# A graph layer on one core: the node layer's own-row product is made early, and two node batches are in flight at the end

## The chip, the cores and the metric

The kernel runs on one core of a Trainium2 chip. A core has a matrix engine (PE, with PEld as the name for its weight loads), a vector engine (DVE), a scalar engine (ACT), a general engine (POOL) and an engine that only issues transfers and waits (SP). Each runs its own instructions strictly in order, and they meet through semaphores. The metric is device time in microseconds, the median of several runs; lower is better.

## The reference

12500 nodes with 64 features, 212500 edges sorted by destination, and one message-passing layer before a residual. The edges are grouped by `row` (the reference's `src` argument) for the sum.

```
h = relu(layernorm(x))                                  # 12500 x 64
edge_in = concat([h[src], h[dst], dist])                # 212500 x 129
e   = silu(edge_in @ eW1 + eb1)                         # 212500 x 128
e   = silu(e @ eW2 + eb2)                               # 212500 x 128
agg = segment_sum(e, src, 12500)                        # 12500 x 128
out = silu(concat([h, agg]) @ nW1 + nb1) @ nW2 + nb2    # 12500 x 64
return x + out
```

The last line but one is the node layer. Its first product has two parts: `h @ nW1[:64]`, which needs only a node's own row, and `agg @ nW1[64:]`, which needs the finished sum.

## The kernel before, in words

All arithmetic on PE is in f32, apart from small helper products. Nodes are laid out as 125 per "bucket" (`L`), 100 buckets (`NB`), and four buckets (`G`) make a batch, so there are 25 batches of 500 nodes. Work runs in these stages:

- **Tables.** `normed`, `turned` and `products` make the normalised rows `h`, transpose them (`hr`), write them to DRAM as `hd` (L678), and write `h @ eW1`'s two halves as tables `ta` and `tb`. These steps are generators; a chain of them called `feed` is advanced a little at a time between other work.
- **Edges, in 208 blocks of 1024.** For each block, `count` finds on DVE and PE the place of every edge, and `send` builds its rows on PE (`qp`, L429), copies them on ACT (`qs`, L439) and scatters them by eight indirect DMAs that POOL issues (L452, 1661 in all) into a DRAM array `q`, sorted by batch and rank.
- **Sweeps.** Once a "level" of ranks is complete in `q`, its 25 batches are swept, one to two steps each, 450 steps in twelve levels. The last four levels have one step a batch. A step loads `qt` (edge rows, L503) and `a` (own rows, L512) through SP, and does on PE: `lr` (L528), `pt` (L542 and L548), `p` (the second layer, L580) and `seg` (the sum over edges, L594). DVE makes one-hot matrices `oneT` (L533) and `one` (L561) and adds `seg` into `aggT` (L605). ACT does the two SiLUs and a bias copy.
- **Tail.** In the last level, `s_add` appends to a list `tails` a generator `nodes(B, ...)` for each finished batch. It does the node layer: `z` on PE from `aggT` (L246) and from the own rows `hrn`, loaded from `hd` (L249), SiLU into `zs` on ACT (L251), `o` on PE (L255), `os` = `o` plus the residual `xr` on DVE (L258), and the store (`rows16`, L120).

PE, DVE, ACT and SP run the order in which the code writes their instructions (`manual_schedule`); POOL's is the planner's. The order of a step is written out in a list, and each `None` in it is a "hook", at which pieces of sending, up to two turns of `feed`, and one turn of the first tail are put in:

```python
turn = [
    (s_pt, 1), (s_add, -2), (s_one_t, 2), None, (s_bias, 1), (s_p2, 0), (s_one, 0), None, (s_seg, -1), None, (s_lr, 3), None,
]
```

The number beside a function says how many steps ahead of the current one, k, it works. So in one step of the last level `z`, `o`, `os` and the store of the batch two back stand at the four hooks.

Loads for batch k+4 are put on SP by `fetch`, called at the end of `s_one(k)`. In the last level `fetch` also calls `nodes_in`, which loads the residual rows `xr` and the own rows `hrn`. `xr` and `hrn` have six buffers each (`nd_in`, `NQ + 2`). A load into a buffer waits on SP until the last reader of its old contents is done, and whatever SP has to issue after it waits too. The PSUM pool `mm` has four buffers, used in turn by `qp`, `lr`, `pt`, `z` and `o`.

Of the kernel before, what the change touches and what calls it, by code (L numbers as in the profile page):

```python
# [28 lines left out]
F32 = mybir.dt.float32  # L29
# [3 lines left out]
AF = mybir.ActivationFunctionType  # L33
OP = mybir.AluOpType
# [4 lines left out]
P = 128  # L39
L = 125  # L40
# [11 lines left out]
G = 4  # L52
# [9 lines left out]
FIRST = 4  # L62
# [11 lines left out]
def tile_gnn(ctx: ExitStack, tc: tile.TileContext, x, src, dst, ew, eW1, eb1, eW2, eb2, nW1, nb1, nW2, nb2, out):  # L74
    nc = tc.nc
# [41 lines left out]
    def rows16(dma, to, of):  # L117

        for part in (slice(0, 112), slice(112, L)):
            dma(to[part], of[part])  # L120
# [86 lines left out]
            nc.scalar.copy(to.rearrange("l (i a) h -> l a i h", a=2)[:, a], abs_[a])  # L207

    hd = dram.tile([P, NB // 2, P], F32, name="hd")
    bkE = const.tile([P, 2 * TB, NP], F32, name="bkE")  # L210
    locE = const.tile([P, 2 * TB, NP], F32, name="locE")
    offE = const.tile([P, 2 * TB, NP], F32, name="offE")
# [17 lines left out]
    def nodes_in(B, sb):  # L230
        b = B * G
        xr = sb.tile([L, G, D], F32, name="xr")
        rows16(nc.sync.dma_start, xr, x_rows[:, b : b + G, :])
        nc.gpsimd.tensor_tensor(xr, xr, nb2b[:L, None, :].to_broadcast([L, G, D]), op=OP.add)
        hr = sb.tile([P, G // 2, P], F32, name="hrn")
        nc.sync.dma_start(hr, hd[:, b // 2 : b // 2 + G // 2, :])
        return xr, hr

    def nodes(B, xr, hr, ps, sb, tag):

        b = B * G

        zs = sb.tile([P, 2, G // 2, L], F32, name="zs")
        z = [ps.tile([P, G // 2, L], F32, name="z", tag=tag) for _ in range(2)]
        for a in range(2):
            nc.tensor.matmul(z[a], w1g, aggT[:, b + a : b + G : 2, :], start=True, stop=False)  # L246
        for a in range(2):
            half = slice(a * D, (a + 1) * D)
            nc.tensor.matmul(z[a], w1n[half, :], hr[half, :, :L], start=False, stop=True)  # L249
        for a in range(2):  # L250
            nc.scalar.activation(zs[:, a], z[a], AF.Silu, bias=nb1c)  # L251
        yield
        o = ps.tile([L, G, D], F32, name="o", tag=tag)
        for t in range(G):
            nc.tensor.matmul(o[:, t, :], zs[:, t % 2, t // 2, :], w2n, start=True, stop=True)  # L255
        yield
        os_ = sb.tile([L, G, D], F32, name="os")
        nc.vector.tensor_tensor(os_, o, xr, op=OP.add)  # L258
        yield
        rows16(nc.sync.dma_start, out_rows[:, b : b + G, :], os_)  # L260


    NQ = 4
# [5 lines left out]
    with ExitStack() as work:  # L269
# [496 lines left out]
        def scale(p0, p1):  # L766

            v = bkE[:, :, p0:p1]

            q4 = lp.tile([P, 2 * TB, p1 - p0], F32, name="q4", tag=f"q4{p0}")  # L770
            nc.vector.tensor_scalar(q4, v, 0.5 - G / 2 - 1.0, 1.0 / G, op0=OP.add, op1=OP.mult)
            nc.vector.tensor_scalar(q4, q4, float(3 * 2**22), None, op0=OP.add)
            yield
            nc.vector.tensor_scalar(q4, q4, -float(3 * 2**22), None, op0=OP.add)
            nc.vector.scalar_tensor_tensor(offE[:, :, p0:p1], q4, float(ROWS * G - G), v, op0=OP.mult, op1=OP.add)
            scaled.update(range(p0, p1))
# [36 lines left out]
        with tc.tile_pool(name="lists", bufs=1, side="right") as lp:  # L813
            x0 = lp.tile([P, NE, D], F32, name="x0")
            x0_rows = x[: NE * P, :].rearrange("(j p) d -> p j d", p=P)
            nc.sync.dma_start(x0[:, :G, :], x0_rows[:, :G, :])
            srcR = lp.tile([NP, PAIR], I32, name="srcR")
            dstR = lp.tile([NP, PAIR], I32, name="dstR")
            f, sf = (lp.tile([NP, PAIR], F32, name=n) for n in ("f", "sf"))
            srcE = lp.tile([P, 2 * TB, NP], F32, name="srcE")  # L820
            fv = f.rearrange("p (g e) -> p g e", e=QR)
            lo = lp.tile([NP, 2 * NQR], F32, name="lo")
            steps15 = lp.tile([P, 2 * NQR], F32, name="steps15")
            nc.vector.tensor_scalar(steps15, nodes1[:, : 2 * NQR], 1.0, float(STEP), op0=OP.subtract, op1=OP.mult)
            rowsD = lp.tile([NP, NQR, 2, QR], BF16, name="rowsD")
            nc.vector.memset(srcR[96:NP, LAST:], N)
            vec = lambda v, lo_, n, m: bass.AP(tensor=v.tensor, offset=v.offset + lo_, ap=[[m, n], [1, m]])
            for to, v, queue in ((dstR, dst, nc.scalar), (srcR, src, nc.sync)):
                for p0, p1 in ((0, 96), (96, NP - 1)):
                    queue.dma_start(to[p0:p1, :], vec(v, p0 * PAIR, p1 - p0, PAIR))  # L830
                queue.dma_start(to[NP - 1 : NP, :LAST], vec(v, (NP - 1) * PAIR, 1, LAST))
            last = bass.AP(tensor=dst.tensor, offset=dst.offset + E - FEW, ap=[[PAD, 1], [0, PAD // FEW], [1, FEW]])
            nc.scalar.dma_start(dstR[NP - 1 : NP, LAST:].rearrange("p (r e) -> p r e", e=FEW), last)
            root = lp.tile([1, 1], F32, name="root")
            nc.scalar.activation(root, ones[:, :1], AF.Sqrt)
            nc.sync.dma_start(x0[:, G:, :], x0_rows[:, G:, :])
            extra_rows(nc.sync.dma_start)
            near, far = norm(x0[:, :G, :], G, True), norm(x0[:, G:, :], NE - G)
            places, table = destinations(), first_rows(0)
            next(near)  # L840
            next(places)
            list(near)
            next(table)
            next(places)
            nc.scalar.copy(sf[:, :BLK], srcR[:, :BLK])
            list(table)
            nc.scalar.copy(sf[:, BLK:], srcR[:, BLK:])
            list(places)
            load_rows(0)
            load_rows(1)  # L850
            next(far)
            list(by_edges())
            list(sources(0, FIRST))
            list(scale(0, FIRST))
            load(0)
            counting = count(0)
            next(counting)
            todo = groups()
            list(counting)
            load(1)  # L860
            for _ in range(2):
                list(todo.pop(0))
            sending = send_all(0, 2 * FIRST)
            feed = itertools.chain(far, *(first_rows(g) for g in range(G, NE, G)))
            for _ in range(2 * PIECES):
                next(sending)
                for _ in range(2):
                    next(feed, None)
            list(feed)
            windows(1)  # L870
            feed = itertools.chain(sources(FIRST, NP), scale(FIRST, NP), checks(), turns(todo, 3))
            for _ in sending:
                for _ in range(4):
                    next(feed, None)
# [31 lines left out]
        for k in range(first, len(steps) + 2):  # L906
            for s in turn:
                if s is None:
                    while len(marks) > 1 and at >= marks[1][0]:
                        marks.pop(0)  # L910
                    if len(marks) > 1:
                        (t0, n0), (t1, n1) = marks[:2]
                        goal = n0 + (n1 - n0) * (at + 1 - t0) / (t1 - t0)
                        while done + 1 <= goal + 0.001:
                            next(pieces, None)
                            done += 1
                    at += 1
                    for _ in range(2):
                        if not ndp and next(feed, 0) == 0:
                            feeding.close()  # L920
                            for name, bufs in (("nd_in", NQ + 2), ("nd", 2)):
                                ndp.append(work.enter_context(tc.tile_pool(name=name, bufs=bufs, side="right")))
                    if tails and next(tails[0], 0) == 0:
                        tails.pop(0)
                else:
                    f, ahead = s
                    if 0 <= k + ahead < len(steps):
                        f(k + ahead)
        for t in tails:
            for _ in t:  # L930
                pass


    flag_i = const.tile([1, 1], I32, name="flag_i")
# [9 lines left out]
    with tc.If(flag > 0):  # L944
        general_sums(tc, N, E, NB, H, src, dst, ew, ta, tb, aggT, w1d, eb1b, w2, ident, ones, eb2r, part)
        with tc.tile_pool(name="fin", bufs=2) as fin, tc.tile_pool(name="fps", bufs=4, space=PSUM) as fps:
            for B in range(NB // G):
                for _ in nodes(B, *nodes_in(B, fin), fps, fin, "fps"):
                    pass


def general_sums(tc, N, E, NB, H, src, dst, ew, ta, tb, aggT, w1d, eb1b, w2, ident, ones, eb2r, part):
# [120 lines left out]
```

## Time and profile before

| what | us |
|---|---|
| median of three runs (lowest, highest) | 2463.26 (2462.79, 2467.51) |
| the profiled execution, its own time | 2461.7 |
| its span, first to last instruction | 2459.9 |
| PE busy in the span | 2045.2 (83%) |
| DVE busy | 1936.9 (79%) |
| POOL busy | 1705.5 (69%) |
| ACT busy | 1088.8 (44%) |

The profiled execution's time and its span differ by 1.8 us, and it is 1.6 us below the median of the runs. A share of busy time is a mean over stages that have different limits, so the stages have to be looked at one by one. PE's busy time includes matmuls that overlap in its pipeline. The mean granted PE clock was 0.92 over the span and 1.00 in the stretches after 1600 us.

### The profile page before, as it was taken

What the parts mean: (1) busy time and instruction counts of PE and PEld (TensorE: products, weight loads), DVE (VectorE), ACT (ScalarE), POOL (GpSimd) and SP (SyncE); (2) the same over time, 40 slices, a digit from 0 to 9 for tenths busy, and PEclk for the clock granted to TensorE, in tenths of its full rate; (3) what the DMA queues carried; (4) which work ended last, traced back from release to release, by engine and by line L of the source; (5) the groups of instructions that cost most, each with busy time, mean ns of one, the idle gap of its engine ahead of it and who ended that gap; (6) DMA issues with size and microseconds to landing.
All of it is one profiled execution on the core that took longest, in us unless ns stands there. A gap on an engine that the chain in (4) does not pass through costs nothing.

```text
span 2459.9 us, 46292 instructions
## 1 busy us (share of the span) xinstructions
PE 2045.2 (83%) x16191; PEld 1829.8 (74%) x16191; DVE 1936.9 (79%) x3006; ACT 1088.8 (44%) x2403; POOL 1705.5 (69%) x1712
## 2 busy tenths in 40 slices
PE   3673776665688898898998988899999999999997
PEld 2452665555587787787887877888888898999986
DVE  7895777676787898787888788898889899886432
ACT  2452333222344454454544444454555555554442
POOL 4777777777777777777777777777777777762110
PEclk9575898877899999999999998999999999999999
DMA  4563566555666765667654544455555556665652
GB/s 116 185 217 124 168 186 193 183 175 171 210 212 211 219 210 180 215 215 227 194 166 165 166 156 161 154 182 165 177 172 181 179 166 207 215 199 174 193 162 67
DMA packets 237006, 443.85 MB, mean 180 GB/s; under 512 B 49804, under 2 KB 108735, under 8 KB 236561
## 3 DMA queue, kind: packets, MB, share of 16 engines
q1 hardware_dynamic: 158629, 269.79, 35.9%
q0 software_dynamic: 53536, 123.03, 14.3%
q10 hardware_dynamic: 24602, 47.98, 6.7%
q8 instruction: 132, 2.16, 0.4%
q14 instruction: 107, 0.88, 0.1%
HBM read 251.07 MB, written 189.55 MB: 179 GB/s over the span
## 4 chain that ended last, share of the span: by engine, by line
PE 36%; DMA 17%; DVE 16%; POOL 13%; issue 8%; ACT 2%; DVEq 0%; POOLq 0%; ACTq 0%; SPq 0%
DMA q<-qs,to 16%; POOL q L452 13%; PE seg L594 8%; PE pt L548 8%; PE p L580 7%; PE pt L542 4%; PE qp L429 4%; DVE oh L354 2%; DVE each L362 2%; DVE oneT L533 2%; PE lr L528 2%; DVE aggT L605 2%; DVE one L561 2%; DVE mine L404 1%; DVE rank L406 1%
## 5 line engine op out<-in xcount | busy, mean ns | idle before, releaser
L452 POOL DMA_INDIRECT q<-qs,to x1661 | 1676.4, 1009 | 586.3 <-issue 396.9
L552 ACT ACTIVATE e<-pt 128x512 f32<-128x512 f32 x450 | 268.7, 597 | 849.8 <-PE pt L548 839.2
L594 PE MATMUL seg<-one,e 128*128 128x125 f32 x3600 | 504.0, 285 | 110.2 <-DVE aggT L605 77.7
L594 PEld LDWEIGHTS seg<-one,e 128*128 128x128 f32 x3600 | 456.0, 199 | 140.0 <-issue 84.7
L580 PEld LDWEIGHTS p<-w,e 128*128 128x128 f32 x3600 | 472.3, 197 | 37.4 <-issue 17.8
L548 PE MATMUL pt<-oneT,a 125*128 125x128 f32 (+1 forms) x2400 | 487.1, 338 | 15.3 <-DVE oneT L533 15.3
L580 PE MATMUL p<-w,e 128*128 128x128 f32 x3600 | 494.1, 281 | 0.0
L548 PEld LDWEIGHTS pt<-oneT,a 125*128 125x128 f32 x2400 | 366.9, 200 | 35.4 <-DVE oneT L533 18.2
L439 ACT COPY qs<-qp 128x512 f32<-128x512 f32 x416 | 224.9, 588 | 356.8 <-PE qp L429 310.1
L533 DVE TENSOR_SCALAR oneT<-lr,part 125x512 f32<-125x512 f32 x450 | 335.0, 745 | 43.4 <-PE lr L528 42.8
L362 DVE TENSOR_REDUCE each<-oh 128x100 bf16<-128x800 bf16 x208 | 315.9, 1519 | 7.2
L561 DVE TENSOR_TENSOR one<-nodes,qt 128x500 f32<-128x500 f32 x450 | 302.4, 672 | 0.2 <-issue 0.2
L542 PE MATMUL pt<-ident,qt 128*128 128x128 f32 x1800 | 287.6, 285 | 1.3 <-DVE oneT L533 1.3
L429 PE MATMUL qp<-win,pick 64*128 64x256 f32 x1662 | 266.3, 435 | 24.2 <-DMA pick<-in_edge_weight_dram 9.1
L584 ACT ACTIVATE e<-p 128x512 f32<-128x512 f32 x450 | 268.7, 597 | 28.7 <-PE p L580 28.7
L574 ACT COPY p<-b2f 128x512 f32<-128x512 f32 x450 | 267.2, 594 | 0.0
L605 DVE TENSOR_TENSOR aggT<-aggT,seg 128x500 f32<-128x500 f32 x275 | 184.0, 669 | 65.5 <-PE seg L594 62.7
L408 DVE SCALAR_TENSOR_TENSOR to<-rank,offE 128x8 int32<-128x8 f32 x208 | 36.2, 174 | 251.3 <-DMA q<-qs,to 246.5
L429 PEld LDWEIGHTS qp<-win,pick 64*128 64x128 f32 x1662 | 162.5, 203 | 81.1 <-issue 44.3
L542 PEld LDWEIGHTS pt<-ident,qt 128*128 128x128 f32 x1800 | 200.7, 148 | 21.3 <-issue 13.4
L406 DVE TENSOR_REDUCE rank<-mine 128x8 f32<-128x800 f32 x208 | 205.1, 986 | 7.2
L404 DVE TENSOR_TENSOR mine<-oh,counts 128x800 f32<-128x800 bf16 x208 | 203.9, 980 | 8.3 <-PE counts L389 8.0
(145 smaller groups left out, 1454.3 us busy)
## 6 DMA issues: line engine op xcount, KB each, us to landing
qt<-q SPq DMA_DIRECT2D x150, 576.0 KB
a<-ta SPq DMA_DIRECT2D x300, 256.0 KB
qt<-q SPq DMA_DIRECT2D x150, 288.0 KB
q<-zeros ACTq DMA_DIRECT2D x25, 1080.0 KB
q<-qs,to POOLq DMA_INDIRECT x1661
q<-zeros ACTq DMA_DIRECT2D x10, 1440.0 KB
bc<-dests SPq DMA_DIRECT2D x103, 128.0 KB
win<-tb SPq DMA_DIRECT2D x416, 30.0 KB
```

Of the source, the lines that this page charges most:

```text
L362: nc.vector.tensor_reduce(each, oh.rearrange("p t b -> p b t"), AX.X, OP.add)
L429: nc.tensor.matmul(qps[i][:, t, : n_of[t]], pick[at, t * P : (t + 1) * P], win[at, : n_of[t]], start=True, stop=True)
L452: ins = nc.gpsimd.indirect_dma_start(out=q[:], out_offset=bass.IndirectOffsetOnAxis(ap=to[:k, j : j + 1], axis=0), in_=qs[:k, t, a, :], in ...
L533: nc.vector.tensor_scalar(oneT, st[k].pop("lr")[:L], part1[:L, :], None, op0=OP.is_equal)
L542: nc.tensor.matmul(pt[:, t, :], qt[:, j, :H], ident, is_transpose=True, start=t == 0, stop=False, skip_group_check=True)
L548: nc.tensor.matmul(pt[:, cols, :], a[:L, b, :], oneT[:, cols, :], start=False, stop=True, skip_group_check=True)
L552: nc.scalar.activation(e1, pt, AF.Silu)
L561: nc.vector.tensor_tensor(one.rearrange("p (b j) l -> p b j l", j=n), nodes1[:, None, None, :].to_broadcast(wide), loc[:, tiles[0][1] : ti ...
L574: nc.scalar.copy(p2, b2f)
L580: nc.tensor.matmul(p2[:, t, :], e1[:, t, :], w2, start=False, stop=t == G - 1, skip_group_check=True)
L584: nc.scalar.activation(e2, p2, AF.Silu)
L594: nc.tensor.matmul(item[2][:, b, :], e2[:, t, :], one[:, t, :], start=j < G, stop=j >= G * (n - 1))
```

## The change: what it does

The own-row product leaves the tail. A new generator `node_part` does for each batch: load `hrn` from `hd`, let six turns go by, two matmuls with `w1n` into two PSUM tiles of pool `mm`, two ACT copies to SBUF, and a store to a new DRAM array `zd` a turn later. The 25 generators stand at the end of `feed`, three at a time. In the program's order the first five batches' products come before the first `lr` of the sweeps and the other twenty in the first eighteen steps of 450.

In the tail, `nodes_in` loads `zh` from `zd` (128 x 500 f32) in place of `hrn` (128 x 256 f32). `nodes` has `z` from `aggT` alone; at its next turn DVE adds `zh` to the two halves of `z`, and ACT makes one SiLU over both. The result store is put off: `os` goes on a list, and the list is sent after the next batch's `z` matmuls. At each hook only one of the two first tails is advanced, by the parity of the hook, so that a batch takes two steps and two are in flight: in one step the new batch has its `z` at the first hook and its additions and SiLU at the third, and the batch before it has its `o` at the second and its `os` at the fourth.

```diff
+    zd = dram.tile([P, NB // G, 2, G // 2, L], F32, name="zd")
...
-        hr = sb.tile([P, G // 2, P], F32, name="hrn")
-        nc.sync.dma_start(hr, hd[:, b // 2 : b // 2 + G // 2, :])
-        return xr, hr
+        zh = sb.tile([P, 2, G // 2, L], F32, name="zh")
+        nc.sync.dma_start(zh, zd[:, B])
+        return xr, zh
+
+    def node_part(B, ps, sb, tag):
+        b = B * G
+        hr = sb.tile([P, G // 2, P], F32, name="hrn")
+        nc.sync.dma_start(hr, hd[:, b // 2 : b // 2 + G // 2, :])
+        for _ in range(6):
+            yield
+        z = [ps.tile([P, G // 2, L], F32, name="zp", tag=tag) for _ in range(2)]
+        for a in range(2):
+            half = slice(a * D, (a + 1) * D)
+            nc.tensor.matmul(z[a], w1n[half, :], hr[half, :, :L], start=True, stop=True)
+        zh = sb.tile([P, 2, G // 2, L], F32, name="zn")
+        for a in range(2):
+            nc.scalar.copy(zh[:, a], z[a])
+        yield
+        nc.sync.dma_start(zd[:, B], zh)
+        yield
+
+    unsent = []
+
+    def send_out():
+        while unsent:
+            rows16(nc.sync.dma_start, *unsent.pop(0))
...
-        zs = sb.tile([P, 2, G // 2, L], F32, name="zs")
+        zs = sb.tile([P, 2, G // 2, L], F32, name="zs", bufs=3)
...
-            nc.tensor.matmul(z[a], w1g, aggT[:, b + a : b + G : 2, :], start=True, stop=False)
+            nc.tensor.matmul(z[a], w1g, aggT[:, b + a : b + G : 2, :], start=True, stop=True)
+        send_out()
+        yield
         for a in range(2):
-            half = slice(a * D, (a + 1) * D)
-            nc.tensor.matmul(z[a], w1n[half, :], hr[half, :, :L], start=False, stop=True)
-        for a in range(2):
-            nc.scalar.activation(zs[:, a], z[a], AF.Silu, bias=nb1c)
+            nc.vector.tensor_tensor(zs[:, a], z[a], zh[:, a], op=OP.add)
+        nc.scalar.activation(zs, zs, AF.Silu, bias=nb1c)
         yield
...
         nc.vector.tensor_tensor(os_, o, xr, op=OP.add)
-        yield
-        rows16(nc.sync.dma_start, out_rows[:, b : b + G, :], os_)
+        unsent.append((out_rows[:, b : b + G, :], os_))
...
-            feed = itertools.chain(sources(FIRST, NP), scale(FIRST, NP), checks(), turns(todo, 3))
+            later = turns([node_part(B, mm, fp, "mm") for B in range(NB // G)], 3)
+            feed = itertools.chain(sources(FIRST, NP), scale(FIRST, NP), checks(), turns(todo, 3), later)
...
-                    if tails and next(tails[0], 0) == 0:
-                        tails.pop(0)
+                    if tails:
+                        both = tails[at % 2 :: 2][:1] if len(tails) > 1 else tails[:1] * (at % 2)
+                        for t in both:
+                            if next(t, 0) == 0:
+                                tails.remove(t)
...
+        send_out()
```

More of the change, by code (lines that the diff above doesn't have):

```diff
@@ L234, in nodes_in, with nodes @@
         nc.gpsimd.tensor_tensor(xr, xr, nb2b[:L, None, :].to_broadcast([L, G, D]), op=OP.add)
+        zh = sb.tile([P, 2, G // 2, L], F32, name="zh")
[3 more added lines that the diff above has]
+        b = B * G
         hr = sb.tile([P, G // 2, P], F32, name="hrn")
         nc.sync.dma_start(hr, hd[:, b // 2 : b // 2 + G // 2, :])
-        return xr, hr
-    def nodes(B, xr, hr, ps, sb, tag):
+        for _ in range(6):
[14 more added lines that the diff above has]
+            rows16(nc.sync.dma_start, *unsent.pop(0))
+    def nodes(B, xr, zh, ps, sb, tag):
         b = B * G
-        zs = sb.tile([P, 2, G // 2, L], F32, name="zs")
+        zs = sb.tile([P, 2, G // 2, L], F32, name="zs", bufs=3)
         z = [ps.tile([P, G // 2, L], F32, name="z", tag=tag) for _ in range(2)]
         for a in range(2):
-            nc.tensor.matmul(z[a], w1g, aggT[:, b + a : b + G : 2, :], start=True, stop=False)
+            nc.tensor.matmul(z[a], w1g, aggT[:, b + a : b + G : 2, :], start=True, stop=True)
+        send_out()
+        yield
         for a in range(2):
-            half = slice(a * D, (a + 1) * D)
-            nc.tensor.matmul(z[a], w1n[half, :], hr[half, :, :L], start=False, stop=True)
-        for a in range(2):
-            nc.scalar.activation(zs[:, a], z[a], AF.Silu, bias=nb1c)
+            nc.vector.tensor_tensor(zs[:, a], z[a], zh[:, a], op=OP.add)
+        nc.scalar.activation(zs, zs, AF.Silu, bias=nb1c)
         yield
@@ L949, in tile_gnn @@
                     pass
+            send_out()
 def general_sums(tc, N, E, NB, H, src, dst, ew, ta, tb, aggT, w1d, eb1b, w2, ident, ones, eb2r, part):
```

## The prediction

> **What bounds the kernel now.** I read the page's head, then busy time by stretch, then what POOL waits for, then the timeline of one step of the tail, and last what SP waits for and which transfers the chain of waits names.
>
> The profiled execution took 2461.7 us, 1.8 over its span and 1.6 under the median; I work in its time and put the difference on the median. About 0.2% (5 us) is what a measurement of this kernel can tell from no change.
>
> The stretches (columns: us, then busy us and count of PE, PEld, DVE, ACT, POOL, then granted clock, DMA share, GB/s):
>
> ```profile
> 250.00:500.00 250.00, 173.53 (x1243) 154.44 (x1245) 183.52 (x278) 83.72 (x190) 191.45 (x193) 0.84 0.59 182
> 1800.00:2000.00 200.00, 192.53 (x1597) 176.35 (x1596) 178.85 (x271) 105.24 (x226) 153.42 (x153) 1.00 0.54 174
> 2200.00:2285.00 85.00, 83.91 (x790) 82.02 (x789) 56.58 (x93) 41.43 (x83) 22.27 (x23) 1.00 0.58 178
> 2304.00:2428.00 124.00, 124.00 (x1011) 109.47 (x1011) 49.59 (x86) 51.08 (x105) 15.21 (x21) 1.00 0.51 153
> ```
>
> PE is idle 30% of the stage where the new work goes (250 to 500) and never in the tail (2304 to 2428). Early, POOL decides. Its waits in 240 to 450:
>
> ```profile
> POOL q L452 <- issue: 39.0, 128, 0.3
> POOL q L452 <- DMA q<-qs,to: 4.0, 13, 0.3
> ```
>
> The last number is the longest wait: 0.3 us. Each scatter takes 1.009 us and that 0.3, and one follows the next until 2201 us. In this stage DVE waits for scatters to finish, not the reverse (column of waits: `to` L408 on the scatter, 41.1 us in 250 to 450). So up to 2201 POOL sets the time, and PE work added early is paid for only if it starves POOL. After that PE sets it alone.
>
> One step of the tail:
>
> ```profile
> 2342.75 0.98 PE L255 MATMUL o<-w2n,zs 128*125 128x64 f32 x8
> 2343.82 0.42 DVE L258 TENSOR_TENSOR os<-o,xr 125x256 f32<-125x256 f32 x1 [3.08 <-issue]
> 2344.28 0.78 SPq L120 DMA_DIRECT2D xr<-in_x_dram  x2
> 2344.51 0.39 PE L528 MATMUL lr<-identb,qt 128*125 128x128 bf16 x4
> 2344.74 0.61 PE L542 MATMUL pt<-ident,qt 128*128 128x128 f32 x4
> 2345.18 1.06 PE L548 MATMUL pt<-oneT,a 125*128 125x128 f32 x8
> 2345.54 0.87 SPq L120 DMA_DIRECT2D out_dram<-os  x2
> 2346.08 1.01 PE L246 MATMUL z<-aggT,w1g 128*128 128x250 f32 x4
> 2346.66 0.34 SPq L503 DMA_DIRECT2D qt<-q  x1
> 2347.02 0.30 PEld L249 LDWEIGHTS z<-hrn,w1n 64*128 64x128 f32 x4 [0.32 <-issue]
> 2347.64 0.97 PEld L580 LDWEIGHTS p<-w,e 128*128 128x128 f32 x8 [0.32 <-issue]
> 2348.64 0.98 PE L255 MATMUL o<-w2n,zs 128*125 128x64 f32 x8
> 2349.45 1.11 PE L594 MATMUL seg<-one,e 128*128 128x125 f32 x8
> 2350.40 0.39 PE L528 MATMUL lr<-identb,qt 128*125 128x128 bf16 x4
> ```
>
> Start to start on PE: `lr` 0.23, `pt` 0.44 and 0.90, `z` from aggT 0.94, `z` from own rows 0.62, `p` 1.00, `o` 0.81, `seg` 0.95: 5.89 us a step. On both sides of L249 the weight load sits idle 0.32 us.
>
> **Part 1, the own-row matmuls leave the tail.** A step loses L249's 0.62 and what hangs on it. `z` from aggT streams 500 columns; `pt` L548 streams 512 in 0.90, so 0.88 in place of 0.94. `p` took 1.00 because `o` waited for `zs` (ACT ends at 2347.74 + 0.83 = 2348.57, `o` starts 2348.64); in the steps before the tail the same eight instructions take 0.90. New step: 0.23 + 0.44 + 0.90 + 0.88 + 0.90 + 0.81 + 0.95 = 5.11. A plain step without node work is 3.35 (chain of waits, `pt` L548 at 2218.76 and 2222.10); 3.35 + 0.88 + 0.81 = 5.04. I take 5.07, a gain of 0.82. There are 20 gaps of 5.89 and one of 5.65 between the 25 `z`: 21 x 0.82 = 17.2. The last three gaps (5.26, 5.36, 5.22) are a chain `z`, `p`, `o`, `seg`, `aggT`, `z`: the first two lose about 0.8 each, the third 1.4, since there `o` also waited 0.6 for `zs`. Together 20.2 us.
>
> A rule speaks against this part. The Trainium skill, "TensorE: Matmul & The Clock Gate", Part 3 (The mechanism), says that matmuls on different row groups run concurrently, and the two of L249 sit on rows 0 to 63 and 64 to 127. By it they would cost 250 columns together, an estimate of 0.44 us, and the gain would shrink by some 4 us; the row says 0.62, and I keep the row.
>
> **Part 2, the same matmuls early.** 25 batches cost PE 0.62 each, and up to 0.64 more if both idle stretches come along: 15.5 to 31.5 us; ACT 50 copies near `rows_a` L207 (378 ns for 128 x 256), 18.9 us. SP issues 25 loads and 25 stores more; what stands behind them is `qt`, `win` and `bc`, loaded blocks ahead. What hides all this is POOL's unbroken scatter stream. I take 0, the nearest evidence being the 0.3 us rows; if the cover fails entirely it is 31.5 us. A gain is excluded, since POOL has as many scatters as before.
>
> **Part 3, additions and SiLU in the tail.** DVE gets two additions over 250 columns from PSUM, near `os` (0.42 each): with `aggT` 0.68, `oneT` 0.75, `one` 0.67 and `os` 0.42 that is 3.4 of 5.07 us. ACT goes from 0.60 x 3 + 0.83 to 0.60 x 4. Neither fills the step, and `o` now reads a `zs` made a step earlier, so nothing on PE waits for them; without that step of room `o` would wait 0.84 + 0.6 a step. The end of the chain (`z`, additions, SiLU, `o`, `os`) trades 0.62 + 0.83 for 0.84 + 0.60: 0.
>
> **Part 4, SP waits longer.** This is the price of two batches in flight. A new `xr` waits for the `os` of six batches before:
>
> ```profile
> SPq L120 <- DVE os L258: 45.3, 18, 2.6
> ```
>
> That is 2310 to 2415: 2.5 us in each step. In the code `os` of batch k-2 moves from step k to the last hook of step k+1, while `xr` for k+4 is still put on SP in step k. So SP stands a step longer, and behind it are `zh`, the stores, and `qt` and `a` for k+5, so far issued right after `one`. They now go out after `os`: 0.04 to the first `xr`, 2.13 to the end of the stores (2344.28 to 2345.54 + 0.87), 0.09: `qt` is issued 2.26 us after `os` ends. `lr` of the next step reads it, 0.27 + 5.07 = 5.34 us after `os` (2344.24 to 2344.51, and a step). So 3.08 us are left for the landing L. The chain of waits shows three:
>
> ```profile
> 2232.94 2.83 DMA qt<-q
> 2272.32 3.16 DMA qt<-q
> 2284.88 4.90 DMA qt<-q
> ```
>
> A lasting lateness is shared by two steps, since a stalled `lr` also delays the next `os`: each step grows by (L - 3.08) / 2. L = 2.83 costs 0, 3.16 costs 0.04 a step, 4.90 costs 0.91, some 20 us in all. The load `zh` adds 128 KB a step, so (288 + 256 + 128 + 250 + 125) KB in 5.07 us, about 210 GB/s against 153 now; 2285 to 2304 already ran at 224. I take 0.1 a step, 2.5 us, since the tail's transfers are spread out and 2.83 is nearest. Bounds 0 and 20. While the first batches of the level are loaded, zh's extra 0.77 MB at 224 GB/s could cost 0 to 3.4; I take 0, as `qt` is issued ahead of it.
>
> By the Trainium skill, "DMA: Bandwidth & Descriptors", Anatomy of one DMA (written for transfers that GpSimd issues) and Bandwidth, a transfer has about 2.0 us fixed and 436 GB/s at best; with 288 KB that is an estimate of 2.7 us for L and no stall at all, which the 4.90 row does not let me lean on.
>
> **Sum.** -20.2 + 0 + 0 + 2.5 = -17.7: the median goes to 2445.6.
>
> **Rivals.**
> - *SP binds the tail, still faster.* L near 4: 0.46 x 21 = 9.7 us back, 3.4 at the start: 2456. For it: the late `qt`. Against it: only one long landing is in the chain.
> - *SP binds the tail, slower.* The same wait of `lr` for `qt`, decided at L = 4.72, where a step is 5.89 again; at 5.2 a step is 6.13 and the time about 2468. For it: 4.90 was seen, at 224 GB/s. Against it: no step of the tail waits for `qt` now.
> - *The early work is not hidden.* If POOL starves for half of PE's 31.5 us: 2461; for all: 2477. For it: SP already waits on `one` in this stage, and the stores stand in its line. Against it: POOL's backlog, DVE waiting for scatters.
> - *The gain is not there*, because additions or SiLU are late and `o` still waits: a step near 5.7, 2459. Against it: the half-filled DVE and ACT.
>
> **How the numbers follow.** Forecast 0.70 (2440 to 2451); SP binds, faster 0.14; SP binds, slower 0.04; early not hidden 0.07, half of it slower and some of the rest within 0.2%; gain not there 0.05. Faster than 2458.3 is then about 0.86, the same 0.07, slower 0.07. The range 2439 to 2457 takes in the forecast with a step of 5.04 and no stall, 2442, and some 3 us for terms too small in my favour; at the other end the first rival.
>
> **What would show it.** Right: the `z` of the tail 5.05 to 5.2 us apart with no L249 between them; PE busy throughout; POOL's waits at 0.3 through 240 to 450 and the last dense scatter near 2201; SP's wait on `os` over 4 us a step. Wrong: `lr` with idle time behind `qt` in most steps (Part 4); POOL waits over 1 us or a first last-level step later than 2304 (Part 2); `o` with idle time behind `zs` (Part 3).

## The result, and the profile after

The changed kernel takes 2453.77 us (median of 7 runs, 2452.58 to 2456.51), against 2462.87 (7 runs, 2459.59 to 2467.51): a ratio of 0.9961, with a 95% interval of 0.9948 to 0.9973. That is 9.1 us faster, half of what was forecast, and inside the range. The profiled execution took 2453.77 us with a span of 2452.0.

In the first two of the three groups of runs below, made on other chips than the third, every kernel took some 24% longer for a reason that was not found, the one before included (3059 us); ratios are formed inside a group only, and the tail's step is the same in all groups.

The stretches, with the columns of the prediction:

```profile
250.00:500.00 250.00, 185.13 (x1316) 156.64 (x1316) 184.28 (x278) 95.72 (x228) 191.45 (x193) 0.85 0.68 212
...
2304.00:2428.00 124.00, 111.26 (x914) 106.42 (x912) 66.42 (x127) 47.90 (x84) 16.37 (x20) 0.97 0.60 165
```

Early, PE is 11.6 us busier (173.53 to 185.13) and POOL exactly as busy as before. In the tail, where PE had no idle time at all, it is now idle for 12.7 of 124 us. POOL's waits in 240 to 450 are the same 0.3 us at the longest, its largest group being:

```profile
POOL q L477 <- issue: 39.6, 130, 0.3
```

The tail's idle time has one name; the largest group of PEld's waits between the first and the last `z` (us in total, times, longest; all others come to 2.9 us):

```profile
PEld L553 <- DMA qt<-q: 14.5, 13, 2.7
```

The timeline shows it with its cause:

```profile
2342.60 0.34 SPq L528 DMA_DIRECT2D qt<-q  x1
...
2345.03 0.42 DVE L284 TENSOR_TENSOR os<-o,xr 125x256 f32<-125x256 f32 x1 [1.35 <-PE o L281]
2345.48 0.78 SPq L120 DMA_DIRECT2D xr<-in_x_dram  x2
2346.31 0.34 SPq L237 DMA_DIRECT2D zh<-zd  x1
2346.62 0.44 PE L553 MATMUL lr<-identb,qt 128*125 128x128 bf16 x4 [0.73 <-DMA qt<-q]
...
2347.67 0.34 SPq L528 DMA_DIRECT2D qt<-q  x1
...
2352.68 0.44 PE L553 MATMUL lr<-identb,qt 128*125 128x128 bf16 x4 [0.78 <-DMA qt<-q]
```

SP stands until `os` ends at 2345.45, then issues `xr`, `zh`, the stores, and 2.22 us after `os` the `qt` that the `lr` of the next step needs. Issued at 2342.60 it is read 4.02 us later, issued at 2347.67 it is read 5.01 us later, with PE idle before it each time. Before, the same distance from the issue of `qt` to its `lr` was 9.63 us in nearly every step.

The 24 gaps between the 25 `z` were 5.89 twenty times, and 139.3 us in all, before. Now they are 4.19, then five of 5.07 among fourteen of 5.25 to 9.26, and at the end 4.83, 4.53, 4.51, 3.65: 135.65 us. So the tail gained 3.7 us in the profiled execution.

### The profile page after: what moved, and what is told of

Its sections match the earlier page's. It is cut to its first block, busy times and chain, and to the rows that moved or that the text cites. A ratio compares the mean times of both kernels' runs of the same rounds, so it can differ in the third digit from the quotient of the medians.

```text
span 2452.0 us, 46508 instructions
## 1 busy us (share of the span) xinstructions
PE 2050.8 (84%) x16191; PEld 1835.4 (75%) x16191; DVE 1958.4 (80%) x3056; ACT 1100.8 (45%) x2428; POOL 1700.7 (69%) x1712
## 4 chain that ended last, share of the span: by engine, by line
PE 36%; DMA 18%; DVE 17%; POOL 12%; issue 8%; ACT 2%; DVEq 0%; SPq 0%; POOLq 0%; ACTq 0%
DMA q<-qs,to 15%; POOL q L477 12%; PE seg L619 8%; PE pt L573 8%; PE p L605 7%; PE qp L454 4%; PE pt L567 4%; DMA qt<-q 3%; DVE oneT L558 3%; PE lr L553 2%; DVE oh L379 2%; DVE one L586 2%; DVE each L387 2%; DVE aggT L630 2%; DVE mine L429 1%
## 5 line engine op out<-in xcount | busy, mean ns | idle before, releaser
L605 PEld LDWEIGHTS p<-w,e 128*128 128x128 f32 x3600 | 471.1, 195 | 31.2 <-issue 13.4
L605 PE MATMUL p<-w,e 128*128 128x128 f32 x3600 | 489.1, 280 | 0.0
```

The costliest lines, as they stand in the source:

```text
L605: nc.tensor.matmul(p2[:, t, :], e1[:, t, :], w2, start=False, stop=t == G - 1, skip_group_check=True)
```

## The experiments

They are told by question. The runs were made in three groups: e1 to e4, e5 to e8 and e9 to e12.

**Is it SP's wait for the old buffer? One and two more buffers.** With seven `nd_in` buffers, `xr` for batch k+4 waits for the `os` of batch k-3, which ended a step earlier; with eight it is two. Nothing else changes.

```diff
-for name, bufs in (("nd_in", NQ + 2), ("nd", 2)):
+for name, bufs in (("nd_in", NQ + 3), ("nd", 2)):   # e10; e1 and e6: NQ + 4
```

> The changed kernel with eight buffers in place of six for xr and zh, so that no xr load has to wait for the os of an unfinished batch. Theory A (SP stands behind that wait, and qt goes out late): the z of the tail come 5.07 us apart throughout, SP's wait on os is gone, lr no longer waits for qt; the tail's 16 us of stalls come back, some 2438 us. Theory B (the tail's transfers themselves are too slow now, zh being twice as large as hrn): qt still lands late, steps stay near 5.8 us, some 2452 us.

> The changed kernel itself, beside the three below. Theory A (a landing of over 4 us for qt, since zh is loaded just ahead of it): ratio to before about 0.996, as in the first measurement; some of the 24 gaps between the z of the tail at 5.07, most at 5.4 to 6.5, lr waiting for qt.

> The changed kernel with nd_in at NQ + 4 buffers in place of NQ + 2, now beside the changed kernel. Theory A: gaps of 5.07 throughout, so 12 to 17 us less than the changed kernel in the tail: ratio to before near 0.990 where the whole takes some 2460 us. If the stalls were only a part of the loss, the tail is as regular but the time stays within 5 us of the changed kernel's.

> The changed kernel itself, beside the three below. Theory A: as in its earlier profiles, the z of the tail between 5.07 and 9 us apart, some 136 us from the first to the last; the time 0 to 9 us under before.

> The changed kernel with seven nd_in buffers (NQ + 3), one more than as given. Theory A: xr for batch k+4 then waits for the os of batch k-3, which ended a step earlier, so SP does not stand, qt goes out right after one, and the tail is as with eight: gaps of 5.07, 118 us from first to last z. Rival (a step's worth of room is not enough, since SP still stands for part of a step): gaps between 5.07 and 5.6 in places, 120 to 128 us.

| run | ratio to before (95%) | first to last `z` | median us |
|---|---|---|---|
| as given, e5 | 0.9999 (0.9966 to 1.0033) | 133.1 | 3058.66 |
| eight buffers, e1 | 0.9947 (0.9917 to 0.9978) | 118.0 | 3049.21 |
| eight buffers, e6 | 0.9939 (0.9909 to 0.9970) | 118.0 | 3039.81 |
| as given, e9 | 0.9955 (0.9939 to 0.9971) | 132.7 | 2450.75 |
| seven buffers, e10 | 0.9903 (0.9883 to 0.9923) | 118.0 | 2441.11 |

One more buffer is enough. After a first gap of 4.20 every gap of e10's tail is 5.07 up to the last four, and PE waits for no `qt`. The change as given shows no gain in e5, where 0.996 was expected. Its tail is as much shorter there as in e9; a cost of the early part in that group (below) may take it back, which is not shown. From the timeline of e10:

```profile
2349.13 0.34 SPq L528 DMA_DIRECT2D qt<-q  x1
...
2352.01 0.39 PE L553 MATMUL lr<-identb,qt 128*125 128x128 bf16 x4
...
2353.57 1.01 PE L272 MATMUL z<-aggT,w1g 128*128 128x250 f32 x4
2354.20 0.34 SPq L528 DMA_DIRECT2D qt<-q  x1
...
2357.08 0.39 PE L553 MATMUL lr<-identb,qt 128*125 128x128 bf16 x4
```

`qt` goes out at the same place in the step, but for a batch one later: the one issued at 2349.13 is read at 2357.08, 7.95 us on. Its landing takes 3.9 us (median) here, little less than in the kernel as given, and nobody waits. SP itself still stands for `os`, against the expectations of e1 and e10: 13.5 us in sixteen waits in e1, and in e10:

```profile
SPq L120 <- DVE os L284: 36.7, 20, 3.4
```

So what the buffer buys is not an SP that never waits, but a `qt` that is issued one step further ahead of its reader.

This stretch also moves more (columns as above):

```profile
2304.00:2420.00 116.00, 115.14 (x997) 112.77 (x996) 71.49 (x138) 51.81 (x91) 16.05 (x22) 1.00 0.69 195
```

At 195 GB/s PE stands for under 1 us, against 12.7 at 165 GB/s as given. Bandwidth was not the limit; the moment of issue was.

**What makes the landing long: `zh`?** First without its load; the additions then read `aggT` in its place, so the own rows' part of the output is left out.

```diff
-zh = sb.tile([P, 2, G // 2, L], F32, name="zh")
-nc.sync.dma_start(zh, zd[:, B])
-return xr, zh
+return xr, None
...
-nc.vector.tensor_tensor(zs[:, a], z[a], zh[:, a], op=OP.add)
+nc.vector.tensor_tensor(zs[:, a], z[a], aggT[:, b + a : b + G : 2, :], op=OP.add)
```

> The changed kernel with six buffers and its late qt, but zh is not loaded: the additions take aggT in its place, so the own rows' part is missing from the result. It measures what the 250 KB of zh ahead of qt cost. Theory A with zh as the cause of the long landing: qt lands in 2.9 us after its issue as in the kernel before, steps are 5.07 to 5.2 us, some 2438 to 2441 us. If the long landing has another cause (the stores, other bytes in flight), qt still takes about 4.2 us and the time stays near 2450 us.

Measured 3041.38 us, ratio 0.9929 (0.9897 to 0.9962): gaps of 5.07 but for one of 5.53. With `zh` away, `qt` goes out half a microsecond earlier and is read 3.60 us after its issue in nearly every step. PE's waits in its tail, all of them:

```profile
PE lr L551 <- DMA qt<-q: 0.3, 1, 0.3
```

So six buffers are just enough when 250 KB less stand ahead of `qt`. Then with `zh`, but laid out so that one batch's rows lie together:

```diff
-zd = dram.tile([P, NB // G, 2, G // 2, L], F32, name="zd")     # zd[:, B]
+zd = dram.tile([NB // G, P, 2, G // 2, L], F32, name="zd")     # zd[B]
```

> The changed kernel, six buffers, with zd laid out batch first, so that the 128 rows of one batch's zh lie behind each other in DRAM, not 50,000 B apart. Theory A (zh's bytes stand ahead of qt, whatever their layout): the gaps as in the changed kernel, mostly 5.4 to 6.5, the time within 3 us of it. Theory A2 (zh's packets are slow because they are far apart, mean 137 ns against 85 for a's): zh and qt land some 1 us sooner, lr hardly waits, gaps of 5.07 to 5.3, 10 to 15 us less.

Measured 3056.9 us, ratio 0.9999 (0.9969 to 1.0029), 132.0 us from first to last `z` against 133.1 as given. PE's waits for `qt` in the tail of this run, and then of the kernel as given beside it:

```profile
PE lr L553 <- DMA qt<-q: 9.7, 10, 2.1
```

```profile
PE lr L553 <- DMA qt<-q: 11.2, 10, 3.0
```

The distance between rows has nothing measurable to do with it; the load itself has. The traces of the other runs bear this out, and show that it matters how near the load stands. Landings of `qt` in the tail, from its issue to its last event (`xr` and the stores are there in every run):

| run | load ahead of `qt` | issued ahead of it by, us | mean landing, us |
|---|---|---|---|
| before, e11 | `hrn`, 128 KB | 1.5, 1.3 | 2.94, 2.95 |
| e4 | neither | | 2.94 |
| as given: first profile, e9 | `zh`, 250 KB | 1.36, 1.36 | 4.36, 4.19 |
| e10, seven buffers | `zh`, 250 KB | 1.6 | 4.05 |
| e1, e6, eight buffers | `zh`, 250 KB | 3.3, 3.3 | 3.20, 3.17 |

**Each half of the change alone.** Two in flight, with both products of `z` left in the tail:

```diff
 # on the kernel before
-zs = sb.tile([P, 2, G // 2, L], F32, name="zs")
+zs = sb.tile([P, 2, G // 2, L], F32, name="zs", bufs=3)
...
+        send_out()
+        yield                      # after the four products of z
...
-        yield
-        rows16(nc.sync.dma_start, out_rows[:, b : b + G, :], os_)
+        unsent.append((out_rows[:, b : b + G, :], os_))
... and the two-batch turn of tails, as in the change
```

> The kernel before with two batches of the node layer in flight, and nothing else of the change: both products of z stay in the tail, hrn (128 KB) is loaded, not zh (250 KB). By the forecast's Part 1, o no longer waits for zs, which is worth the 0.10 by which p was late: steps of 5.79, so 2 us in all, and in the chain after the last step some 0.6 more. By Part 4's sum lr then has 0.27 + 5.79 - 2.26 = 3.80 us for the landing of qt, and with 128 KB ahead of it Theory A expects no or few stalls. Rival (SP's later stand alone costs, whatever is loaded behind it): gaps of 6 us and more in many steps.

Measured 2461.95 us, ratio 0.9995 (0.9982 to 1.0008). The steps are 5.89, as before, not 5.79; one gap is 6.43. `qt` is read 3.94 us after its issue, and only one `lr` waits; PE's waits in its tail, all of them:

```profile
PE lr L536 <- DMA qt<-q: 0.3, 1, 0.3
```

The expected absence of stalls came, the 0.10 did not. The timeline shows why:

```profile
2356.15 0.97 PEld L588 LDWEIGHTS p<-w,e 128*128 128x128 f32 x8 [0.32 <-issue]
2356.15 1.16 PE L588 MATMUL p<-w,e 128*128 128x128 f32 x8
2357.15 0.98 PE L264 MATMUL o<-w2n,zs 128*125 128x64 f32 x8
2357.84 0.82 ACT L260 ACTIVATE zs<-z,nb1c 128x250 f32<-128x250 f32 x2
```

`o` at 2357.15 reads a `zs` from a step earlier, since this step's SiLU comes after it, and `p` still takes 1.00 from start to start. The 0.10 is therefore not a wait for `zs`; it goes with the 64-row weights of the own-row product just ahead of `p`, behind which the weight load sits idle 0.32 us. The rival is out: a late SP by itself costs nothing at this step length, with 128 KB ahead of `qt`.

Then the early product with one batch in flight:

```diff
-if tails:
-    both = tails[at % 2 :: 2][:1] if len(tails) > 1 else tails[:1] * (at % 2)
-    for t in both:
-        if next(t, 0) == 0:
-            tails.remove(t)
+if tails and next(tails[0], 0) == 0:
+    tails.pop(0)
```

> The changed kernel with the early product kept, but the first tail alone is advanced at every hook as before, so that one batch is in flight and its os falls in the step of its z. Theory A: xr waits less than a step, qt is not late; a step is 5.07 us if o does not wait for zs (2438 us) and up to 5.55 us if zs stands behind the second SiLU of ACT (2450 us). Theory B: qt is late as in the changed kernel, some 2452 us.

Measured 3062.24 us, ratio 1.0023 (0.9992 to 1.0053). The steps are 5.68 throughout, more than the 5.55 allowed for, since `o` waits in each for `zs`:

```profile
PE o L281 <- ACT zs L277: 7.9, 20, 0.4
```

So neither half gains 2 us by itself: from the first to the last `z` e11 is 1.0 us shorter than before and e2 1.8. The rival "the gain is not there" describes e2 well; in the changed kernel it is two batches in flight that keep `o` from waiting.

**Is the early part free?** The kernel before with `zd`, `node_part` and the `later` turns of the change; `zd` is never read, and the tail is as before.

```diff
+later = turns([node_part(B, mm, fp, "mm") for B in range(NB // G)], 3)
-feed = itertools.chain(sources(FIRST, NP), scale(FIRST, NP), checks(), turns(todo, 3))
+feed = itertools.chain(sources(FIRST, NP), scale(FIRST, NP), checks(), turns(todo, 3), later)
```

> The kernel before with the 25 early products, their loads and stores added and the tail left as it was; zd is written and never read. Theory A (hidden behind POOL's scatters): 2463 us, within 3 us of the kernel before, and the first z of the tail at 2301 to 2305 us. Rival (the early part moves the time by itself, as the first z of the changed kernel came 4.1 us sooner): 2459 us or less, or, if it is not hidden, 2470 us or more.

> Again the kernel before with the 25 early products made and stored as in the changed kernel but never read, the tail as before. The forecast's Part 2 (hidden behind POOL's scatters): within 3 us of before. Rival (not hidden): 15 to 31 us more.

> Once more the kernel before with the 25 early products made and stored, never read. If the cost seen so far (0.28% and 0.26%, each within its interval of nothing) is real, it is again 0.2 to 0.4%, 5 to 11 us; if the work is hidden, the three together lie within 0.1% of before.

Measured 3070.72 us, ratio 1.0028 (0.9997 to 1.0058); 3069.21, 1.0026 (1.0000 to 1.0051); and in the third group 2462.42, 0.9991 (0.9980 to 1.0003). POOL's waits in 240 to 450 go with it. In the third run first, where the stream of scatters is unbroken, then in the first, where ACT's `qs` comes late:

```profile
POOL q L471 <- issue: 39.6, 130, 0.3
```

```profile
POOL q L471 <- ACT qs L464: 25.3, 7, 5.4
POOL q L471 <- ACT zn L253: 14.1, 6, 3.1
```

Where POOL's stream is unbroken the work is hidden: e12 leaves room for a cost of 0.7 us at most. In the two slower groups POOL stands for ACT, and the second row names ACT's copies of the early product itself (`zn`). There the point value of both runs is 8 us or a little more, of the 15.5 to 31.5 that the work takes. Each interval reaches to nothing or nearly so, but the two together do not (1.0027, by an estimate from both intervals 1.0007 to 1.0047). So the early part is probably not free there, as the condition named in the prediction, an unbroken stream, would have it; without a profile of the kernel before in those groups this is not shown.

## Why the prediction was right, and where not

**Part 1, right, with a wrong reason in it.** The unstalled step is 5.07. In e10: `lr` 0.23, `pt` 0.44 and 0.89, `z` 0.86, `p` 0.88, `o` 0.82, `seg` 0.95. Without stalls the tail gains 139.3 - 118.0 = 21.3 us, against 20.2; the difference is the first gap, 4.20, because no `o` falls into it yet. The 0.10 of `p` was put down to a late `zs`; e11 shows that it hung on L249. It left with L249, so the sum held. With the 0.44 that I drew from the rule on row groups the step would have been left at about 5.26 (4 us over 21 steps more); the row decided, and its 0.62 was the right number. But the row does not speak against the rule, as the prediction has it. The trace's single records of the step that the prediction shows have L249's four matmuls starting in pairs 7 ns apart (2347.017 and 2347.024, then 2347.334 and 2347.341 us), so the two row groups do run at the same time. Two passes at the spacing of `z` from `aggT` (0.21 us) are 0.42. The other 0.2 of the 0.62, and the 0.10 on `p`, go with weight loads that start together with their first matmul, and not ahead of it (2347.02 and 2347.64).

**Part 2, right where POOL's stream is unbroken.** POOL's waits are as before, and e12 measures the part alone at nothing; in the slower groups some 8 us are likely. PE's added 11.6 us in 250 to 500 lay in idle time. The sign named for this part, a last level that starts no later than 2304, could not have decided: the first `z` came at 2300.7, 2307.0, 2308.8 and 2305.8 in the profiles of the change, e9, e10 and e12, and at 2304.8 and 2302.4 in those of before and e11, which have no early work.

**Part 3, right.** The two additions took 0.77 us together and one SiLU 0.70; `o` hardly waits. From the last `z` to the end of the span it is 15.7 us before and after, so the 0 for the end of the chain held too.

**Part 4, the mechanism right, its size wrong: this is the step that failed.** The delay of `qt` behind `os` was forecast as 2.26 us and is 2.22; the room of 3.08 is 0.27 + 5.07 - 2.22 = 3.12. Wrong was L, and with it the 0.1 us a step that I took for the stall. I took 2.83, from a stretch in which `qt` had no load ahead of it, on the argument that the tail's transfers are spread out. For the kernel before that was a fair figure: in its own tail, with the 128 KB of `hrn` ahead, 19 landings have a mean of 2.94 us (2.73 to 3.74). What I put at nothing is that the load ahead becomes twice as large. In the changed tail 18 landings have a mean of 4.36 us (3.08 to 5.88). The trace ends each transfer in 16 events: the first comes 2.6 to 3.2 us after the issue, the last 0.5 to 3.1 us after that one, where before it was 0.3 to 1.2. `zh` (250 KB) is issued 1.36 us ahead and itself takes 3.0 us, so it is still under way in the first 1.7 us of `qt`'s landing. Its bytes I had counted as bandwidth, and found enough; that they lie in front of the one transfer without room was the point. (`zh` is 122 KB larger than `hrn`, not 128 as the prediction says; nothing hangs on it.) The 2.7 us estimated from the Trainium skill, "DMA: Bandwidth & Descriptors", is near the median of 2.82 in the tail before, and far from the 4.36. The same page, Why a DMA increments its semaphore by 16 and not by 1, says that up to 16 engines finish independently; the 16 events agree, and it is the last of them that `lr` waits for.

By the formula of the prediction a mean of 4.36 costs (4.36 - 3.08) / 2 = 0.64 in each of 21 steps, 13.4 us. Measured were 135.65 - 118.0 = 17.6: 14.5 us of waits (the PEld line above) and some 2.8 of something that I had not thought of, a slower PE after the longest wait (below). So -21.3 + 17.6 = -3.7 in this execution; the first rival, "SP binds the tail, still faster", is the case that came, at 2454 for its 2456. I had named it and given it 0.14. That the time lies inside the range, and so near 2456, is in part luck: the stalls cost 17.6 us where that rival had 9.7, and the 3.7 us of the profiled tail alone would have left 2459, outside the range.

**A sign that was badly chosen.** SP's wait for `os` was to exceed 4 us a step. It is 2.9 us in each of 17 steps, against 2.5:

```profile
SPq L120 <- DVE os L284: 49.7, 17, 6.7
```

The wait begins later as well, because `qt` and `a` are now issued just ahead of it. The distance from the issue of `qt` to its `lr` (9.63, then 4 to 5) would have been the sign to name.

**What stays open.** The profiled tail accounts for 3.7 of the 9.1 us (6.6 of 13 in e9). The first `z` lies anywhere from 2300.7 to 2308.8 in profiles of kernels with the same work up to there, so single profiles cannot place the rest; that executions without a profile stall less is possible and not shown. Which of the 16 parts of `qt` comes late, and behind what, was not looked into.

**A better version.** e10 beats both: 2441.11 us, 22.6 below before in its group and 9.6 below the change as given, for one buffer more.

## What to carry to other kernels

Before a step is shortened or shifted, measure for each load in it the time from its issue to its first reader, and look at which loads stand in the same queue ahead of it; a step that is 0.8 us shorter takes that from every load's room. Where a queue is in order, a buffer that is reused a step later delays all that is issued behind it: one spare buffer was worth about as much here as the whole change as given. Compare the room with a landing measured beside the neighbours that the load will have, not those it has: behind 128 KB `qt` landed in 2.9 us, behind 250 KB as near in 4.4, and behind the same 250 KB issued 3.3 us ahead in 3.2. Price the spread of landings, not only their median.

## What the runs showed of the hardware that was not expected

**A wait of 2.5 us on PE costs more than itself.** At the longest wait the granted clock (the first figure after POOL's columns), 1.00 until then, halves, and stays so through the 5.5 us of the second row:

```profile
2330.00:2333.00 3.00, 0.45 (x5) 0.28 (x4) 0.67 (x1) 0.00 (x0) 0.00 (x0) 0.80 0.59 148
2333.00:2338.50 5.50, 5.50 (x26) 5.18 (x26) 2.52 (x4) 1.09 (x2) 0.72 (x1) 0.50 0.53 165
2338.50:2345.00 6.50, 6.50 (x58) 6.40 (x58) 3.12 (x6) 3.13 (x6) 0.73 (x1) 0.99 0.41 97
```

```profile
2332.72 0.69 PE L553 MATMUL lr<-identb,qt 128*125 128x128 bf16 x4 [2.55 <-DMA qt<-q]
...
2335.76 1.87 PE L272 MATMUL z<-aggT,w1g 128*128 128x250 f32 x4
```

PE idles for 2.55 us, and then `z` takes 1.87 us in place of 1.01. Lost are 1.45 us in this gap (9.26 - 5.07 - 2.74) and 1.38 in the next (6.45 - 5.07). In e9 a wait of 2.2 us was followed by the same, the clock at 0.62 and 0.81 in the next two stretches of 3 us. The length of the wait does not decide alone: in e7 one of 2.1 us was followed by a lower clock (0.68 and 0.75), but in the first profile another of 2.1 us, which ended at 2371.12, was not, nor were the shorter ones:

```profile
2369.00:2372.00 3.00, 0.89 (x11) 0.88 (x11) 1.08 (x2) 0.00 (x0) 0.00 (x0) 1.00 0.64 160
2372.00:2375.00 3.00, 3.00 (x27) 2.90 (x25) 1.71 (x4) 1.41 (x3) 1.14 (x1) 1.00 0.73 207
```

The Trainium skill, "TensorE: Matmul & The Clock Gate", Part 1, lets the clock halve after an idle window of about 3.4 us; here waits of 2.1 to 2.6 us could be enough.
